# An attention and mixture-of-experts layer: the router's last steps, the order of its sends, and the last batch's additions re-timed

## The chip, the cores and the metric

The kernel runs on one core of a Trainium2 chip. The time is that of the whole program on the device, in microseconds (us); of the kernel before, three runs gave a median of 751.35 us (750.44 to 752.04). Five engines work side by side, each through its own instructions in a fixed order: PE multiplies matrices, DVE and ACT and POOL work on vectors, SP issues transfers. PE writes its products into PSUM; the others work in SBUF and PSUM; DMA moves rows between SBUF and the memory outside. An engine waits at an instruction until what it needs is there, and all that stands behind it on that engine waits too.

## The reference

The input `x` holds 16 batches of 512 rows of 128 numbers. With `xn = layernorm(x)` the output is `x + attention(xn) + experts(xn)`.

```python
q, k, v = heads of xn@Wq, xn@Wk, xn@Wv          # 16 heads of 8 numbers
q, k = q/|q|, k/|k|
attn = softmax(causal(8 * q k^T))
attention = (attn v) @ Wo

probs = softmax(xn @ Wr^T)                      # 8 experts
top_v, top_i = top_k(probs, 2); top_v /= sum(top_v)
experts = sum over e of  w_e * (gelu(xn @ W1[e]^T + b1[e]) @ W2[e]^T + b2[e])
```

Here `w_e` is the weight that a row gives to expert `e`, zero if it is not one of the row's two. All numbers are 32-bit floats.

## The kernel before, in words

**The stages of attention.** A batch's attention goes in 10 stages (`PER`), so that the program has stages 0 to 159 (`PER * B` = 160), and stage t belongs to batch t // 10. In each stage PE makes the scores of four heads at once (`scores`, L727), ACT takes the exponentials (L737), POOL or DVE sets to zero what lies above the diagonal (`mask`), and two stages later (`LAG`) PE weighs the values with them (`weigh`, L771) into `av`, the one PSUM buffer for it. After four stages in ten, at t % 5 of 4 and 1, DVE transposes `av` into SBUF (L783); the next weighing writes the same buffer and waits for that. `prep` has the steps that make the next batches' queries and keys (among them L624 `proj`, L683 `qT`, L690 `kr`, L696 `kT`), and `finish` those behind the weighing: division by the sums (L798, L800), a transpose (L810), the product with `Wo` into `po` (L815), the addition to `x` (L819). `prep`, `finish` and others enter their steps in `plan` under a stage number. The products that need one small PSUM buffer (`misc`: `proj`, the turned `q` and `k`, `po`, idle products) share it, one at a time.

**The order of the work.** PE, SP, DVE and ACT execute in the order in which the program's text issues instructions, and `on_pool` holds POOL to the same. `stage(t, b, n)` issues, in this order: at most two sends, the scores, a step of `side`, the masks of the stage before, the weighing, and then `due(t)`: the steps of `plan` for t, the router's steps whose stage has come, one of the steps in `later`, and calls of `combine`.

**The router.** From stage 20 on `route` and `place` run as 19 steps on DVE, with a product or a few on PE: the best and second-best expert of each row, their weights, and for each of the two choices the position at which the row is to lie among its expert's rows. The table of stages ahead of `stage` names them by index: 7 to 9 are `exps`, `shares` and `gates` (which writes the weights into the last columns of the rows), 10 to 16 are `taken`, `count`, `starts`, `ends`, `earlier`, `slot` and `moved`, 17 and 18 are `choose(0)` and `choose(1)`, which write the positions. Behind them come 13 steps in `later` (`ended`, `owners`, `own`, `bias`, `biased`), which find out which expert owns which block of rows; one goes at each stage with t % 10 of 3, 4 or 8.

**The sends.** From stage 40 on POOL sends the rows to `slots`, in the memory outside: 128 indirect transfers of 128 rows, 13 in each batch's ten stages (line 565 is the helper's, for all that POOL does).

**The experts.** Behind stage 139 (`FIRST` = 14 batches) the 71 blocks of rows are fetched, multiplied (L884, L897), weighted and scattered to `results`. Batch 13 is weighed to its end beside the first of them, and batch 14 begins behind the last.

**The last two batches.** From stage 140 on attention goes on for batches 14 and 15. Between, SP loads the experts' results of each batch (`bring`, into buffers called `xnT` and `yt`), `combine(b)` adds them to `x` on DVE in two additions of 128x512 (L983), and `store` sends a batch to `out` when both the attention's and the experts' share have been added. `late` lists the batches that wait for `combine`; `due` starts them by a rule of t: from stage 145 one per stage, two at 148, 153 and 158, none at 151. After stage 159, two more stages (160, 161) weigh what is left, each with one idle product (`keep_busy`, L1031, 128x384 of the weights `wall`, whose result nobody reads), then four idle products follow, and the last batch's division, transpose, product, addition and store.

## Time and profile before

| what | value |
|---|---|
| median of three runs | 751.35 us (750.44 to 752.04) |
| the profiled execution | 748.66 us |
| its span in the profile | 747.0 us |
| PE, DVE, ACT, POOL busy | 716.7, 474.0, 469.0, 475.1 us |
| weighing that waits for DVE's transpose (L783), after us 130 | 6.5 us in 7 waits |
| POOL's sends (128, line 565, `slots<-rows,pos`) | 149.8 us |
| attention up to the experts; experts; the last two batches | to about 425; about 425 to 687; about 687 to 747 us |

The page's times are microseconds from the start of the span. PE, DVE, ACT and POOL are the engines; SP issues transfers. A line such as `734.27 1.48 PE L771 MATMUL av<-ex,vaug 128*12 128x512 f32 x16 [1.93 <-DVE mid L783]` reads: from 734.27 us on, for 1.48 us, PE ran 16 passes for line 771 of the kernel, which write `av` and read `ex` and `vaug`; before that it stood idle for 1.93 us, until DVE's line 783, which writes `mid`, was done. A 32-bit product is two passes. Matmuls are pipelined and their ends are modelled. The profiled execution is one; its own time stands beside the median of the other runs.

### The profile page before, as it was taken

The page shows a single profiled execution, that of the slowest core. Times are in us where ns is not written, and L with a number is a line of the kernel's source. Part 1 is how long each engine was busy: PE and PEld are TensorE (multiplying, and loading weights), DVE is VectorE, ACT ScalarE, POOL GpSimd, SP SyncE. Part 2 cuts the span into 40 slices and gives each one's busy share as a digit, 9 for nine tenths or more (in the row PEclk, how much of TensorE's full clock was granted, in tenths as well). Part 3 has the DMA queues.
Part 4 walks back from the last instruction along what each step waited for, and adds up shares of the span by engine and source line. Part 5 has one row for each costly group of instructions (what it writes and reads, how often), then busy time and mean ns, then how long its engine had stood idle before and what let it go on. Part 6 is the DMA issues. An engine that isn't in the chain of part 4 may idle for free.

```text
span 747.0 us, 17437 instructions
## 1 busy us (share of the span) xinstructions
PE 716.7 (96%) x6411; PEld 437.9 (59%) x6411; DVE 474.0 (63%) x1045; ACT 469.0 (63%) x732; POOL 475.1 (64%) x565
## 2 busy tenths in 40 slices
PE   6899999989999999999999899999999999999996
PEld 2344544334444344444444489999899999998442
DVE  6875578897877876667666645554545554444694
ACT  3677677768887788788888734444343444446872
POOL 4658355478898888888888436554545455455542
PEclk9999999999999999999999999999999999999999
DMA  9930000001101101111110488878778877871992
GB/s 264 342 126 2 1 1 2 1 21 37 35 30 35 37 32 33 38 33 34 35 37 31 133 259 248 238 239 235 226 209 235 241 236 225 248 214 35 296 328 58
DMA packets 90358, 95.38 MB, mean 128 GB/s; under 512 B 10765, under 2 KB 67984, under 8 KB 90274
## 3 DMA queue, kind: packets, MB, share of 16 engines
q1 hardware_dynamic: 80994, 76.93, 35.4%
q0 software_dynamic: 8416, 17.06, 6.7%
q8 instruction: 51, 0.84, 0.5%
q10 hardware_dynamic: 864, 0.28, 0.2%
q14 instruction: 33, 0.27, 0.1%
HBM read 63.87 MB, written 30.82 MB: 127 GB/s over the span
## 4 chain that ended last, share of the span: by engine, by line
PE 78%; DVE 11%; POOL 6%; issue 3%; DMA 1%; ACT 1%; DVEq 0%; POOLq 0%; ACTq 0%
PE sim L727 16%; PE av L897 16%; PE av L771 16%; PE ph L884 16%; PE proj L624 5%; POOL slots L565 3%; PE xgt L861 2%; DVE x L983 2%; PE po L815 2%; PE idle L1031 2%; DMA xnT<-results 1%; POOL ex L565 1%; DVE mid L783 1%; PE qt L681 1%; PE xnt L296 1%
## 5 line engine op out<-in xcount | busy, mean ns | idle before, releaser
L737 ACT ACTIVATE ex<-sim 128x1024 f32<-128x1024 f32 x320 | 310.0, 1022 | 89.3 <-PE sim L727 86.3
L565 POOL DMA_INDIRECT results<-y,to x135 | 132.6, 982 | 132.7 <-DVE y L905 108.9
L888 ACT ACTIVATE gT<-ph,bias 128x256 f32<-128x256 f32 x284 | 108.5, 465 | 150.5 <-PE ph L884 145.4
L727 PE MATMUL sim<-qT,kT 32*128 32x512 f32 (+3 forms) x2048 | 189.6, 460 | 0.5 <-ACT ex L737 0.5
L771 PE MATMUL av<-ex,vaug 128*12 128x512 f32 (+3 forms) x2048 | 168.2, 435 | 8.0 <-DVE mid L783 7.3
L565 POOL DMA_INDIRECT slots<-rows,pos x128 | 149.8, 1171 | 29.5 <-issue 25.8
L565 POOL TENSOR_SCALAR_AFFINE_SELECT ex<-ex 128x512 f32<-128x512 f32 (+1 forms) x139 | 113.9, 826 | 78.6 <-ACT ex L737 73.1
L727 PEld LDWEIGHTS sim<-qT,kT 32*128 32x128 f32 x2048 | 95.8, 183 | 77.2 <-issue 34.3
L897 PE MATMUL av<-xnT,gT 128*128 128x128 f32 x1080 | 132.4, 275 | 0.9 <-ACT gT L888 0.9
L884 PE MATMUL ph<-xgT,xnT 128*128 128x256 f32 (+1 forms) x568 | 129.0, 370 | 2.3 <-DVE xgT L864 2.3
L897 PEld LDWEIGHTS av<-xnT,gT 128*128 128x128 f32 x1080 | 126.3, 192 | 2.5 <-ACT gT L888 1.9
L771 PEld LDWEIGHTS av<-ex,vaug 128*12 128x12 f32 x2048 | 42.4, 91 | 118.8 <-issue 82.8
L884 PEld LDWEIGHTS ph<-xgT,xnT 128*128 128x128 f32 x568 | 99.2, 191 | 13.3 <-DVE xgT L864 2.9
L783 DVE STREAM_TRANSPOSE mid<-av 128x512 f32<-128x512 f32 x64 | 45.7, 714 | 62.5 <-PE av L771 62.3
L864 DVE COPY xgT<-xgt 128x256 f32<-128x256 f32 x71 | 29.2, 411 | 63.4 <-PE xgt L861 63.4
L902 DVE TENSOR_TENSOR y<-av,bb 128x256 f32<-128x256 f32 x71 | 29.2, 411 | 63.0 <-PE av L897 60.8
L624 PE MATMUL proj<-wall,xnT 128*128 128x384 f32 x128 | 57.6, 536 | 6.4 <-DVE xnT L297 2.9
L749 DVE TENSOR_TENSOR ex<-ex,causal 128x1024 f32<-128x1024 f32 (+1 forms) x43 | 53.8, 1252 | 4.7 <-ACT ex L737 4.6
L565 POOL TENSOR_TENSOR qkn<-qkv 128x256 f32<-128x256 f32 x64 | 42.8, 677 | 10.7 <-ACT qkv L627 10.3
L624 PEld LDWEIGHTS proj<-wall,xnT 128*128 128x128 f32 x128 | 19.3, 188 | 33.1 <-issue 16.3
L696 DVE TENSOR_SCALAR kT<-kr,hmask 128x512 f32<-128x512 f32 x64 | 37.9, 595 | 0.6
L627 ACT COPY qkv<-proj 128x384 f32<-128x384 f32 x64 | 30.9, 482 | 9.7 <-PE proj L624 8.3
(162 smaller groups left out, 553.2 us busy)
## 6 DMA issues: line engine op xcount, KB each, us to landing
xnT<-in_w1T_dram SPq DMA_DIRECT2D x71, 256.0 KB
xnT<-in_w2T_dram SPq DMA_DIRECT2D x71, 256.0 KB
slots<-fill SPq DMA_DIRECT2D x45, 198.0 KB, 5.0
xg<-slots SPq DMA_DIRECT2D x64, 132.0 KB
xnT<-results SPq DMA_DIRECT2D x13, 512.0 KB, 8.5
bb<-in_b_dram SPq DMA_DIRECT2D x71, 64.0 KB, 3.5
x<-in_x_dram SPq DMA_DIRECT2D x16, 256.0 KB, 4.9
out_dram<-x SPq DMA_DIRECT2D x16, 256.0 KB, 4.0
```

Of the source, the lines that this page charges most:

```text
L565: ins = op(*args, **kw)
L624: nc.tensor.matmul(pp[:, :NQKV], xnT[b][:, ts(c, P)], wall, start=True, stop=True)
L627: nc.scalar.copy(s["qkv"][:, c], pp[:, :NQKV])
L696: nc.vector.tensor_scalar_mul(s["kT"][:, r], s["kr"], hmask[:, r : r + 1])
L727: nc.tensor.matmul(halves[g // 2][:, g % 2, col : col + (NC - j) * P], s["kT"][group, r, ts(j, P)], s["qT"][group, j * P :], start=True, s ...
L737: nc.scalar.activation(ex[:, 2 * h : 2 * h + 2], half, AF.Exp, scale=SCALE)
L749: nc.vector.tensor_mul(diag, diag, causal.unsqueeze(1).unsqueeze(1).to_broadcast([P, NG, many, P]),)
L771: nc.tensor.matmul(av[32 * g : 32 * g + VW, j * P :], s["vaug"][:, j, NG * g + r], s[m][:, g, col : col + (NC - j) * P], start=(j == 0), s ...
L783: nc.vector.transpose(s["mid"][:, r], av)
L884: nc.tensor.matmul(ph[:, m], s["w1"][:, ts(m, P)], s["xgT"], start=True, stop=True)
L888: nc.scalar.activation(s["gT"][:, m], ph[:, m], AF.Gelu, bias=bias1[:, i, m : m + 1])
L897: nc.tensor.matmul(py[:, c], s["gT"][:, m, ts(c, P)], s["w2"][:, m], start=(m == 0), stop=(m == NM - 1),)
```

## The change: what it does

- `starts` (step 12) goes at stage 31 instead of 33; `gates` (step 9) at 38 instead of 37. `choose(1)` is no longer a step of the router but the first step of `later`, and is still issued at stage 38; so each of the 13 steps behind it goes one place later (the last at stage 83 instead of 78).
- `choose(k)` enters the 64 sends of its choice. So all the first choices' sends go first, then all the second choices'; before, each tile of 128 rows had both, one after the other. The stages and the number of sends in each are the same.
- The `combine`s have a new rule: from stage 145 one per stage, two at 147 and 159, none at 151 and 158, the last at 160.
- Of the idle products near the end, the one at stage 161 is dropped, and two instead of four stand ahead of the last product.
- For the last batch the addition and the store of the result go in two halves of 256 columns.

The transfers' bytes, the products that count, and what ACT and POOL do are the same.

```diff
             nc.vector.tensor_copy(pos[:, k], at)
-            if k:
-                sends.extend(
-                    lambda k=k, i=i: send(k, i) for i in range(NT) for k in range(2)
-                )
+            sends.extend(lambda i=i: send(k, i) for i in range(NT))
...
         return [
             taken, count, starts, ends, earlier, slot, moved,
-            lambda: choose(0), lambda: choose(1),
-        ], [lambda f=f, k=k: f(k) for k in range(2) for f in (ended, owners)] + [own] + [
+            lambda: choose(0),
+        ], [lambda: choose(1)] + [
+            lambda f=f, k=k: f(k) for k in range(2) for f in (ended, owners)
+        ] + [own] + [
             lambda f=f, m=m: f(m) for m in range(NM) for f in (bias, biased)
         ]
...
             xb = x_sb[b].rearrange("p c d -> p (c d)")
-            nc.vector.tensor_add(xb, po, xb)
-            store(b)
+            if b < B - 1:
+                nc.vector.tensor_add(xb, po, xb)
+                store(b)
+            else:
+                assert b in ready
+                for c in range(0, NC, 2):
+                    part = slice(c * P, (c + 2) * P)
+                    nc.vector.tensor_add(xb[:, part], po[:, part], xb[:, part])
+                    nc.sync.dma_start(
+                        out[b, part].rearrange("(c p) d -> p c d", p=P), x_sb[b][:, c : c + 2]
+                    )
             del live[b]
...
-        late[:0] = [(PER * FIRST + 5, n) for n in range(FIRST)]
+        late[:0] = [(PAIR, n) for n in range(FIRST)]
...
-        (29, (6,)), (30, (11,)), (31, (7,)), (32, (8,)), (33, (12, 13)), (34, (14,)),
-        (35, (15,)), (36, (16,)), (37, (17, 9)), (38, (18,)),
+        (29, (6,)), (30, (11,)), (31, (7, 12)), (32, (8,)), (33, (13,)), (34, (14,)),
+        (35, (15,)), (36, (16,)), (37, (17,)), (38, (9,)),
...
-        if b is None:
+        if t == PER * B:
             keep_busy(1, wall)
...
-        for _ in range(2 if t % PAIR == 3 else t % PER != 1):
+
+        t -= PER * FIRST
+        for _ in range(2 if t in (7, 19) else t not in (11, 18)):
             if late and late[0][0] <= t:
                 combine(late.pop(0)[1])
...
-    keep_busy(4, wall)
+    keep_busy(2, wall)
```

## The prediction

> **What bounds the kernel now.** I read the page first, then the waits of PE, then the timeline round the two places that the change touches: the router's end (us 150 to 160) and the last batch (us 700 to 747).

> The page's first part, and from the waits (engine, line, what it waited for, us in total, times, longest), PE's after us 130:

> ```profile
> PE 716.7 (96%) x6411; PEld 437.9 (59%) x6411; DVE 474.0 (63%) x1045; ACT 469.0 (63%) x732; POOL 475.1 (64%) x565
> ...
> PE av L771 <- DVE mid L783: 6.5, 7, 1.9
> PE proj L624 <- DVE kr L690: 1.6, 1, 1.6
> ```

> PE is the bound almost throughout, so only PE's stalls and the tail behind its last product can be won. DVE causes most stalls: the next weighing (L771) may not write `av` before DVE has transposed it (L783), and DVE's strict order puts other work ahead of that. The largest are these (timeline: start, length, in brackets the idle time before):

> ```profile
> 151.91 0.21 DVE L377 TENSOR_TENSOR sums<-wsel 128x64 f32<-128x64 f32 x1
> ...
> 154.02 0.68 DVE L690 COPY kr<-kt 128x512 f32<-128x512 f32 x1
> ...
> 156.68 0.74 DVE L501 TENSOR_TENSOR past<-iota_b,end 128x568 f32<-128x568 f32 x1
> 157.34 0.71 DVE L783 STREAM_TRANSPOSE mid<-av 128x512 f32<-128x512 f32 x1
> ...
> 154.75 0.91 PE L624 MATMUL proj<-wall,xnT 128*128 128x384 f32 x2 [1.55 <-DVE kr L690]
> 158.19 1.48 PE L771 MATMUL av<-ex,vaug 128*12 128x512 f32 x16 [1.46 <-DVE mid L783]
> ```

> The gates (five instructions from 151.91) hold up `kr`, and `past` holds up the transpose. At the end:

> ```profile
> 728.35 5.15 DVE L983 TENSOR_TENSOR x<-x,xnT 128x512 f32<-128x512 f32 x6
> 733.42 0.71 DVE L783 STREAM_TRANSPOSE mid<-av 128x512 f32<-128x512 f32 x1
> 737.65 0.72 DVE L783 STREAM_TRANSPOSE mid<-av 128x512 f32<-128x512 f32 x1 [3.52 <-PE av L771]
> ...
> 739.25 0.71 DVE L810 STREAM_TRANSPOSE oT<-o 128x512 f32<-128x512 f32 x1
> 742.59 0.69 DVE L819 TENSOR_TENSOR x<-po,x 128x512 f32<-128x512 f32 x1 [2.63 <-PE po L815]
> ...
> 734.27 1.48 PE L771 MATMUL av<-ex,vaug 128*12 128x512 f32 x16 [1.93 <-DVE mid L783]
> ...
> 737.51 3.82 PE L1031 MATMUL idle<-wall 128*128 128x384 f32 x8
> 741.39 1.16 PE L815 MATMUL po<-wo_sb,oT 128*128 128x128 f32 x8
> ```

> Six additions (three of `combine`) delay the transpose at 733.42 by 1.8 us and PE by 1.93. `oT` is ready at 739.96, but the last product starts at 741.39: it stands behind four idle products.

> **The change part by part.** The profiled execution took 748.66 us (span 747.0); the median shown is 751.35, so 2.69 more. I sum against the span and carry the difference to the median.

> *`starts` at stage 31.* Five small instructions, 135.30 to 136.59, 1.3 us, move ahead of L810 and `shares`. DVE runs without a gap from 129.16 to 141.9, so the transpose at 138.94 does not move, nor PE's 0.88 us stall there. What now comes 1.3 us later: `oT`, ready about 133.5, wanted at 136.69; `ss`, ready about 136.7, wanted by ACT at 138.12. Cost 0.

> *Gates behind `kr` and `kT`, `ended(0)` out of stage 38.* `kr` goes at 151.91 (its product ended at 151.5): PE's 1.55 us vanishes. But it then meets the transpose earlier: DVE has the same work before that, less `past`, 156.68 to 157.34. So of 1.55 only 0.66 us stays. POOL's first send waits for the gates: about 155.4 instead of 154.44. Behind it stand the second send, the squares at 158.28 and the masks. The second send now reads a first choice's position and no longer waits for 156.77, so two sends end near 158.1 instead of 158.25, and the rest of POOL's queue is not later. Gain 0.66; ends: 0 (POOL is on the chain from 193 to 244, and PE waits 0.71 for it at 244.00) and 1.0.

> *The other steps one slot later.* At stages 48 and 68 PE lost 0.28 (184.98) and 0.45 us (238.43) to a transpose behind four `owners` instructions (1.65) and one `bias` (1.55). Now one `past` (0.74) and one reduction (0.73) stand there, and a `bias` each moves into 58 and 78, worth 0 to 0.45 each. Between -0.73 and +0.17; I take -0.1, near the middle of new against old stalls.

> *Order of the sends.* 128 as before, at the same places between POOL's instructions, 1.17 us each, the same rows and bytes. SP reads slots only at stage 140. Cost 0; the row that bounds it is the sends' own 0.96 to 1.86 us, whose spread has no tie to the choice that I can see, so 0 with ±0.3.

> *Additions re-timed.* Up to stage 152 DVE's order is the same. At 153 one `combine` less stands before the transpose: it starts at 719.54 instead of 720.86, and PE's 0.51 at 721.71 goes. At 156 PE is the later one. At 159 two `combine`s less stand before it; it goes when PE is through, 731.0 (731.43+0.1, less 0.51 and rounding), ends 731.7, and PE's 1.93 goes: L771 starts at about 731.9, 2.4 earlier. Then the weighings follow, 1.42 and 0.98, with no idle product (0.84) between. POOL's last two masks (1.65 from 732.94) come 0.6 earlier and end at 734.0, so PE ends near 734.5 instead of 737.58.

> But three `combine`s now stand between the last two transposes, where none stood: six additions from 731.65. A pair took 1.32 us undisturbed (732.10 to 733.42) and 1.65 to 2.1 beside a mask (728.35 to 730.45). At 3 × 1.32 plus about 0.6 for the two masks they end at 736.15. So DVE, not PE, ends last: the last transpose starts 1.5 us before its 737.65, not 3.1. Ends: 3 × 1.32 gives 735.6; 3 × 2.1 gives 737.9. I take nearer the quiet rate, since POOL has only 1.65 us of work left.

> *Two idle products instead of four.* From the last transpose's start to `oT`'s end it took 2.31 us; so `oT` is ready at 738.5. PE's two idle products (1.9) end at 736.4, out of the way. The last product starts at 738.5 instead of 741.39: 2.9 us earlier (3.4 and 1.2 at the ends). All PE waits named before are in this sum.

> *Last addition and store in halves.* Both wait for the whole product, as the second addition brings no wait of its own. Two additions of 128x256 at 0.41 (L902's row) against one of 0.69: the second store goes 0.1 later than the one would. The old store took 2.30 us from issue (743.30) to landing (745.60); half the bytes land in between nothing saved and perhaps 0.4 less. Net 0, ±0.3; SP's queue is empty by then.

> Sum: 0.66 + 0.1 + 2.9 = 3.7 us. 747.0 becomes 743.3, the profiled execution about 745.0, the median 751.35 - 3.7 = 747.65; I say 747.7.

> [...] PE's granted clock is 1.00 in all windows to 740 and 0.92 in the last:

> ```profile
> 740.00:747.00 7.00, 2.44 (x12) 1.26 (x10) 0.69 (x1) 0.00 (x0) 0.00 (x0) 0.92 0.14 37
> ```

> 0.08 of 7.00 us is 0.56, at half clock 1.1 us, so the clock falls near 745.9, 3.4 us after PE's last product. At the start, at half clock, two passes of 512 columns took 2.09 us (L1031) against 1.05 later (L403), so a drop would double the last product's 1.16. My sum leaves PE idle for 2.1 us (736.4 to 738.5), about as long as the 1.93 before L771 at 734.27, behind which 16 passes ran at the usual 1.48: no cost. [...]

> The additions beside masks ran 1.00 to 1.47 instead of 0.69, and a mask of 1.08 ran 1.62. [...]

> **Rivals.** (1) *The gain stays in DVE's queue.* The six additions go at 2.1 a pair throughout, the last transpose starts at 737.9 and `oT` is ready at 740.2; the tail wins only 1.2, and if PE's idle time of 3.8 us lowers the clock, the product takes 1.2 more. The front's 0.76 is lost at 244. Then 751.35 - 0 to 1.2, say 750.7. For it: nearly all second additions between 716 and 732 took 1.0 to 1.47. Against: POOL is done by 734. (2) *POOL becomes the bound in front*: the first send is 0.96 later and POOL hands that on to 244, +0.96 instead of -0.76, so 749.4. Against it: POOL waited for ACT at 181.64 and 208.43, so it had caught up. (3) *Slower*: every one of the six additions takes 1.47 (the longest seen). The last transpose starts at 740.4, `oT` is ready at 742.7, PE has idled over 6 us, the product takes 2.3 and ends at 745.0 against 742.55: +2.45 - 0.76, 753.0. Its turning point is 1.23 us an addition, where `oT` is as late as the four idle products made the last product. (4) *The edits do nothing in front*, DVE's stretch staying full: 748.45, inside the forecast's own range.

> **How the numbers follow.** A measurement of this kernel tells about 0.2% (1.5 us) from no change. Forecast, with (4), 746.4 to 749.4: 0.70. (2): 0.08, also faster by over 0.2%. (1): 0.14, within 0.2%. (3): 0.06; other causes of a loss 0.02. So faster 0.78, same 0.14, slower 0.08. The range goes from the quiet additions with a full gain in front (3.4 + 1.0 + 0.5 = 4.9, 746.4) into (1), 750.7.

> **What would show it.** `proj` near 153.2 without a wait for `kr`; L771 at 157.5; no wait of PE for `mid` after 715 over 0.3 us; six additions of 4.0 to 5.2 us ending at 735.6 to 736.8 (0.8 earlier if the front's gain holds); the last product led by `oT`, not by idle products, at 1.16. Wrong I'd be if those additions went over 7 us, if the clock fell before the last product, or if PE's waits for POOL between 160 and 250 grew by over 1 us.

## The result, and the profile after

The changed kernel takes 744.88 us (median of four runs, 744.58 to 746.93) against 750.89 for the kernel before beside it; the ratio is 0.9941 with a 95% interval of 0.9917 to 0.9964, or 4.4 us less (2.7 to 6.2). Put to the 751.35 us of the runs shown, that is 746.9 us against a forecast of 747.7. The medians themselves lie 6.0 us apart, more than the forecast's range allowed; what is known of that rest stands further down. Ratios leave out the few executions that ran over 1.5% longer than the shortest of their kernel (the longest: 1761.92 us of the kernel before, 814.71 us of the one with `choose(1)` at stage 43, below). The profiled execution took 746.93 us, the longest of the four; the one before, 748.66, was shorter than all four runs beside it (748.99 to 752.04). So the spans, 745.2 against 747.0, differ by only 1.8 us.

The first part of its page, and the waits of PE after us 130 (engine, line, what it waited for, us in total, times, longest):

```profile
PE 716.9 (96%) x6405; PEld 438.8 (59%) x6405; DVE 474.8 (64%) x1046; ACT 468.6 (63%) x732; POOL 473.5 (64%) x565
```

```profile
PE av L770 <- DVE mid L782: 3.5, 3, 2.1
...
PE po L814 <- DVE oT L809: 2.0, 1, 2.0
PE av L770 <- POOL ex L564: 1.6, 5, 0.7
```

PE is still the bound. Its waits for `mid` fell from 6.5 us to 3.5, the wait for `kr` is gone, and one is new: the last product waits 2.0 us for `oT`. The router's end (timeline: start, length, idle time before in brackets):

```profile
149.80 0.68 DVE L689 COPY kr<-kt 128x512 f32<-128x512 f32 x1
...
151.02 0.91 PE L623 MATMUL proj<-wall,xnT 128*128 128x384 f32 x2
...
152.71 0.69 DVE L491 TENSOR_TENSOR mine<-xnT,sel 128x512 f32<-128x512 f32 x1
...
154.26 0.71 DVE L782 STREAM_TRANSPOSE mid<-av 128x512 f32<-128x512 f32 x1
...
155.12 2.24 PE L770 MATMUL av<-ex,vaug 128*12 128x512 f32 x16 [2.12 <-DVE mid L782]
```

`kr` now runs ahead of the gates and `proj` waits for nothing. But VectorE (DVE) then works through the gates and, as before, through `choose(1)` (from 152.71) ahead of the transpose, and PE reaches it earlier, so PE's next wait is 2.12 us instead of 1.46. The weighing behind it takes 2.24 us instead of the 1.48 it took before. The end of the last batch:

```profile
731.41 0.72 DVE L782 STREAM_TRANSPOSE mid<-av 128x512 f32<-128x512 f32 x1 [1.04 <-PE av L770]
732.06 4.78 DVE L991 TENSOR_TENSOR x<-x,xnT 128x512 f32<-128x512 f32 x6
...
735.36 1.88 PE L1039 MATMUL idle<-wall 128*128 128x384 f32 x4
...
736.75 0.71 DVE L782 STREAM_TRANSPOSE mid<-av 128x512 f32<-128x512 f32 x1
...
738.34 0.71 DVE L809 STREAM_TRANSPOSE oT<-o 128x512 f32<-128x512 f32 x1
...
739.20 1.89 PE L814 MATMUL po<-wo_sb,oT 128*128 128x128 f32 x8 [1.96 <-DVE oT L809]
741.12 0.76 DVE L825 TENSOR_TENSOR x<-po,x 128x256 f32<-128x256 f32 x2 [2.07 <-PE po L814]
741.58 0.89 SPq L826 DMA_DIRECT2D out_dram<-x  x2
```

The additions no longer delay the transpose at 731.41; it is VectorE that waits now (1.04 us). Six additions stand between the last two transposes and take 4.78 us. The last product is led by `oT`, with the idle products out of the way, but takes 1.89 us instead of 1.16.

Both slow pieces of PE's work lie in a stretch at half clock, as the windows show (stretch, length, then busy us of PE, PEld, DVE, ACT and POOL, each with its count; the granted clock of PE, DMA share, GB/s). The stretches are cut where the clock record changes:

```profile
152.29:155.70 3.41, 1.29 (x16) 0.28 (x12) 3.31 (x9) 2.59 (x4) 2.25 (x2) 1.00 0.06 22
155.70:159.11 3.41, 3.41 (x32) 1.42 (x20) 1.94 (x2) 0.00 (x0) 3.20 (x4) 0.50 0.07 24
...
735.97:739.38 3.41, 1.39 (x4) 0.51 (x4) 2.94 (x6) 0.00 (x0) 0.00 (x0) 1.00 0.29 77
739.38:742.79 3.41, 1.71 (x8) 1.41 (x7) 0.76 (x2) 0.00 (x0) 0.00 (x0) 0.50 0.09 25
```

After a window in which PE was idle for 2.1 and 2.0 of 3.41 us, the clock is half for the next one. A third such window (425.35 to 428.77) follows the experts' first transposes, behind one in which PE was idle for 1.92 us. The kernel before had waits at the same places, but its windows fell otherwise, or the idle time in them was less:

```profile
151.99:155.40 3.41, 1.86 (x26) 0.77 (x18) 3.27 (x9) 1.98 (x3) 2.82 (x4) 1.00 0.03 7
155.40:158.82 3.42, 1.96 (x17) 0.59 (x20) 3.35 (x7) 2.42 (x3) 2.00 (x3) 1.00 0.07 22
...
732.26:735.67 3.41, 1.48 (x17) 0.39 (x16) 1.83 (x3) 0.55 (x1) 1.65 (x2) 1.00 0.31 89
```

Its 1.55 us (for `kr`) and 1.46 us (for `mid`) were in two windows, and the 1.93 us ahead of 734.27 did not lower the clock.

So that the clock's chance windows can be told from the edits, I cut every span at three PE rows: the weighing behind a wait of 0.77 us at 123 to 125 (start of part B), the experts' first transpose `xgt` behind 1.06 us (start of C), and the weighing behind the last batch's wait of 1.0 us (start of D). Part B holds the router's end and all the sends, C the experts, D the last batch's end. The starts in the changed kernel are 123.10, 423.55 and 709.68. "Half" marks a window at half clock in that part.

| | A | B | C | D | span |
|---|---|---|---|---|---|
| before | 124.49 | 300.25 | 284.51 | 37.70 | 747.0 |
| after | 123.10 | 300.44 half | 286.13 half | 35.54 half | 745.2 |

Before and after, C is the same work: 1.62 us is what one half-clock window costs. The sum is -1.39 in A, +0.19 in B, +1.62 in C and -2.16 in D. A has no edit in it; PE's clock became full at 12.04 us before and at 8.93 after, and over all 14 profiles A is longer where that was later (123.1 us for 8.9, 123.5 for 9.6 to 9.9, 124.5 for 12.04). So that is chance too.

### The profile page after: what moved, and what is told of

It reads as the page before. It is cut to its first block, busy times and chain, and to the rows that moved or that the text cites. A ratio compares the mean times of both kernels' runs of the same rounds, so it can differ in the third digit from the quotient of the medians.

```text
span 745.2 us, 17428 instructions
## 1 busy us (share of the span) xinstructions
PE 716.9 (96%) x6405; PEld 438.8 (59%) x6405; DVE 474.8 (64%) x1046; ACT 468.6 (63%) x732; POOL 473.5 (64%) x565
## 3 DMA queue, kind: packets, MB, share of 16 engines
q1 hardware_dynamic: 81010, 76.93, 35.2%
## 4 chain that ended last, share of the span: by engine, by line
PE 84%; DVE 8%; POOL 4%; ACT 2%; issue 2%; DMA 1%; DVEq 0%; POOLq 0%; ACTq 0%
PE sim L726 19%; PE av L770 17%; PE av L905 16%; PE ph L892 16%; PE proj L623 6%; PE po L814 2%; POOL slots L564 2%; PE xgt L869 2%; DMA xnT<-results 1%; PE qt L680 1%; DVE x L991 1%; PE idle L1039 1%; PE kt L687 1%; ACT ex L736 1%; PE xnt L296 1%
## 5 line engine op out<-in xcount | busy, mean ns | idle before, releaser
L564 POOL DMA_INDIRECT slots<-rows,pos x128 | 146.4, 1144 | 29.2 <-issue 25.9
L564 POOL TENSOR_TENSOR qkn<-qkv 128x256 f32<-128x256 f32 x64 | 45.0, 712 | 9.3 <-ACT qkv L626 9.0
```

The source lines that it names most:

```text
L564: ins = op(*args, **kw)
```

## The experiments

**The two halves of the change, and the two parts of the tail.** These ran on another chip, where the experts' part takes 13 to 18 us longer and the times scatter more (the kernel before: 763.54 us, 757.65 to 773.73).

The front alone is the kernel before with the new order of sends, the later steps and the table:

```diff
-            if k:
-                sends.extend(lambda k=k, i=i: send(k, i) for i in range(NT) for k in range(2))
+            sends.extend(lambda i=i: send(k, i) for i in range(NT))
...
-            lambda: choose(0), lambda: choose(1),
+            lambda: choose(0),
+        ], [lambda: choose(1)] + [
...
-        (29, (6,)), (30, (11,)), (31, (7,)), (32, (8,)), (33, (12, 13)), (34, (14,)),
-        (35, (15,)), (36, (16,)), (37, (17, 9)), (38, (18,)),
+        (29, (6,)), (30, (11,)), (31, (7, 12)), (32, (8,)), (33, (13,)), (34, (14,)),
+        (35, (15,)), (36, (16,)), (37, (17,)), (38, (9,)),
```

> Only the router's steps, the sends' order and the later steps are changed; the end is as before. Theory (DVE's order): PE loses its waits for kr and for two transposes, and gains one smaller wait; between us 100 and 420 PE comes 0.7 to 1.6 us ahead of before, and the median is 0.7 to 1.6 us lower, 0.1 to 0.2%. Rival A (the clock's phase makes most of the change): PE's order wins nothing lasting, under 0.4 us at us 420 when windows of half clock are taken out. Rival B (POOL hands its late first send on): PE is 0.3 to 1.0 us later than before at us 250.

The tail alone is the kernel before with the re-timed additions, the idle products and the halves; then come the idle products alone, and the additions alone:

```diff
-    keep_busy(4, wall)
+    keep_busy(2, wall)
...
-        if b is None:
+        if t == PER * B:
```

```diff
-        late[:0] = [(PER * FIRST + 5, n) for n in range(FIRST)]
+        late[:0] = [(PAIR, n) for n in range(FIRST)]
...
-        for _ in range(2 if t % PAIR == 3 else t % PER != 1):
+        t -= PER * FIRST
+        for _ in range(2 if t in (7, 19) else t not in (11, 18)):
```

> Only the last batch's part is changed: additions, idle products, halves; the router is as before. Theory: the last product starts 2.5 to 2.9 us earlier against PE's events at us 700, it is led by the last transpose, and the median falls by 2.2 to 3.0 us, 0.3 to 0.4%; if PE's idle time before the last product falls into a window of the clock, that product takes 1.9 instead of 1.2 us. Rival A (the gain stays in DVE's queue): under 1.5 us.

> Before, with the idle product of stage 161 and two of the last four taken out, nothing else. Theory: in before the last product stood behind the idle products 1.4 us after oT was ready, and one more delayed the last weighing by 0.84, so this alone wins about 2.2 us (the last transpose 0.84 earlier, the last product 0.05 behind oT); with additions moved as well the two gains overlap, since then DVE ends last. If the additions were what counts, under 0.5 us.

> Before, with the additions' stages alone changed; all six idle products stay. Theory: PE's waits of 0.51 and 1.93 go, the six additions end 1.0 to 1.5 us before the last transpose of before, and four idle products end near oT, so this alone wins about 2.2 us, too, and the last product runs at full clock because PE is not idle ahead of it (1.17 us). If the idle products were what counts, under 0.7 us.

| | ratio | 95% | median, us | B | C | D |
|---|---|---|---|---|---|---|
| front | 0.9990 | 0.9961 to 1.0019 | 761.40 | 303.39 half | 302.29 | 37.69 |
| tail | 0.9936 | 0.9909 to 0.9964 | 758.44 | 301.35 | 302.19 | 35.19 half |
| idle products | 0.9962 | 0.9937 to 0.9988 | 761.56 | 302.38 | 298.96 | 35.41 |
| additions | 0.9971 | 0.9938 to 1.0004 | 760.34 | 301.90 | 297.62 | 35.29 |

The times say that the gain is the tail's. They can say little more, since C differs by 5 us between executions without an edit in it. The lead of 0.7 to 1.6 us that the front was to gain is not to be seen: its B is 1.0 to 2.0 us longer than with the front untouched, with a half-clock window of 1.62 in it. Part D says more: the front leaves it at 37.69, and each half of the tail takes 2.3 to 2.4 us from it. Together they take 2.5 here, where the last product lay partly at half clock (1.54 us), so the two overlap for the most part. With fewer idle products only, the additions still delay the transpose, but PE catches up, since no idle product stands between the last weighings, and `oT` leads by 0.70 us:

```profile
749.55 0.71 DVE L783 STREAM_TRANSPOSE mid<-av 128x512 f32<-128x512 f32 x1
750.40 2.34 PE L771 MATMUL av<-ex,vaug 128*12 128x512 f32 x32 [1.92 <-DVE mid L783]
...
755.26 1.13 PE L815 MATMUL po<-wo_sb,oT 128*128 128x128 f32 x8 [0.70 <-DVE oT L810]
```

With the additions only, the wait of 1.93 us is gone, but the last product stands behind four idle products again:

```profile
745.61 1.48 PE L771 MATMUL av<-ex,vaug 128*12 128x512 f32 x16
...
748.84 3.83 PE L1031 MATMUL idle<-wall 128*128 128x384 f32 x8
...
751.67 0.71 DVE L810 STREAM_TRANSPOSE oT<-o 128x512 f32<-128x512 f32 x1
...
752.73 1.16 PE L815 MATMUL po<-wo_sb,oT 128*128 128x128 f32 x8
```

`oT` ends at 752.38 and the idle products at 752.67.

**The changed kernel again, and the clock at its end.** On a quieter chip (the kernel before: 752.22 us) I ran the changed kernel once more, without an edit.

> The changed kernel once more, unaltered, beside three kernels that differ from it in one place each. From the first pair of traces: the stretch from the weighing that follows PE's wait of 1.0 us (first of the last batch's waits for `mid`) to the end of the span, 37.75 us before the change and 35.5 after it, is again 35 to 35.6 us here (35.5 where PE's 1.96 us of idle time ahead of the last product lies in one window of the clock gate, 34.8 where it is split). PE's wait for `mid` behind choose(1) is again 2.1 us. Against the kernel before: 3.5 to 5 us lower. A rival, that the front cost what the tail won, expects less than 2 us.

Measured: 746.32 us, ratio 0.9919 (0.9890 to 0.9947), 5.9 us between the medians, more than the 3.5 to 5 expected; B 301.73 with a half-clock window, C 286.15 with one, D 35.65 with the last product at half clock (2.01 us). D as expected. The wait at the router's end was 2.12 us again, split between two windows this time (1.66 us in one), and no drop followed it; it followed a wait of 1.88 us for POOL at 242.98 instead.

Then one idle product more at the end:

```diff
-    keep_busy(2, wall)
+    keep_busy(3, wall)
```

> The changed kernel with three idle products at the end instead of two. Theory on the clock: the last product ran at half clock (1.87 instead of 1.17 us) because PE was idle for 1.96 us within one 3.41 us window ahead of it. One more idle product (0.95 us) leaves 1.0 us idle; the clock stays full until the last product in every execution, the product takes 1.17 us, and the last product still starts right behind `oT`. The stretch to the end is 34.8 us whatever the phase of the window: 0.7 us less than the changed kernel's where that drops, the same where it does not. Rival: the product was slow for another reason (its eight weights are `oT`, loaded late), and takes 1.87 us again.

Measured: 745.38 us (744.93 to 746.46), ratio 0.9911 (0.9885 to 0.9938), B 300.42 and C 286.14 with a half-clock window each, D 34.78. The end of its timeline:

```profile
735.66 2.85 PE L1039 MATMUL idle<-wall 128*128 128x384 f32 x6
...
738.64 0.71 DVE L809 STREAM_TRANSPOSE oT<-o 128x512 f32<-128x512 f32 x1
739.50 1.13 PE L814 MATMUL po<-wo_sb,oT 128*128 128x128 f32 x8 [0.99 <-DVE oT L809]
```

PE is idle for 0.99 us, the product starts right behind `oT` as before, and takes 1.13 us. D is 0.76 us shorter than after the change and 2.92 shorter than before it. That the clock, and not weights that come late, made it 1.89 us, another profile of the tail shows best. With the sends interleaved (below), PE waits the same 1.96 us for `oT`, but 1.60 of it lie in one window and the rest in the next, the clock stays full, and the product takes 1.13 us:

```profile
747.91 1.13 PE L817 MATMUL po<-wo_sb,oT 128*128 128x128 f32 x8 [1.96 <-DVE oT L812]
```

So the rival is out. In the times, 0.76 us is not to be seen.

**`choose(1)` out of the transpose's way.** It goes at stage 43 instead of 38, and all later steps one place further:

```diff
-        if later and not router and t % PER in (3, 4, 8):
+        if later and not router and t > 38 and t % PER in (3, 4, 8):
```

> The changed kernel, but with choose(1) at stage 43 instead of 38, out of VectorE's work ahead of the transpose of stage 39; ended, owners, bias and biased each go one place later still. My theory, that PE's wait at that transpose grew from 1.46 to 2.12 us because `choose(1)` stands ahead of it (1.55 us): the wait becomes 0.5 to 0.7 us, no half-clock window can follow it, and the span is 1.5 us shorter than the changed kernel's, up to 3.1 where that one's wait fell into one clock window. Rival: the weighing then waits for POOL (masks behind sends) or the later stages' transposes give the 1.5 us back by us 270: no difference to the changed kernel within 0.5 us.

```profile
153.60 0.71 DVE L782 STREAM_TRANSPOSE mid<-av 128x512 f32<-128x512 f32 x1
...
154.45 1.48 PE L770 MATMUL av<-ex,vaug 128*12 128x512 f32 x16 [0.57 <-DVE mid L782]
```

Measured: 743.06 us, ratio 0.9881 (0.9852 to 0.9911); B 299.67 and C 284.51, neither with a half-clock window, and D 35.50, with the last product at half clock (1.84 us). The wait is 0.57 as expected, and the weighing takes 1.48 us again. But of the 1.55 us, and of the window of 1.62 that no longer follows, B keeps 0.77 against the first profile of the changed kernel, 2.06 against the second. Its waits for POOL between 128 and 300 tell where the rest went:

```profile
PE av L770 <- POOL ex L564: 3.3, 5, 1.1
```

They were 1.2 in the first profile of the changed kernel and 2.8 in the second: PE, earlier by the wait that it no longer has, meets the masks behind POOL's sends. So both theories hold a part. The profiled execution took 745.37 us, though; four others took 743.00 to 743.08, below all six of the changed kernel beside them (743.95 to 749.38). Where those four are shorter was not traced.

**The last additions spread as well**, on top of `choose(1)` at 43:

```diff
-        for _ in range(2 if t in (7, 19) else t not in (11, 18)):
+        for _ in range(2 if t == 7 else t != 11):
```

> As the kernel with choose(1) at stage 43, and the last additions spread so that one `combine` each goes at stages 158, 159 and 160, where the changed kernel has none at 158 and then one and two more behind. Theory: VectorE stood idle for 1.04 us ahead of the transpose at 731.4, so a pair of additions (1.35 us) there puts PE's wait for that transpose up by 0.3 us and the last transpose down by 1.0 us; `oT` is ready 1.0 us earlier, PE is idle for 0.5 to 1.0 us ahead of the last product, which goes at full clock (1.17 us). The stretch from the first weighing of the waits named above to the end is 34.0 to 34.6 us instead of 35.5; in all 2.5 us below the changed kernel (1.8 to 4.0). Rival: the added pair meets a mask of POOL and takes 2.1, the transpose is late by 1.1, and nothing is won at the end.

```profile
728.59 0.70 DVE L782 STREAM_TRANSPOSE mid<-av 128x512 f32<-128x512 f32 x1
...
729.45 2.42 PE L770 MATMUL av<-ex,vaug 128*12 128x512 f32 x32 [0.59 <-DVE mid L782]
...
732.59 0.71 DVE L782 STREAM_TRANSPOSE mid<-av 128x512 f32<-128x512 f32 x1
...
735.04 1.13 PE L814 MATMUL po<-wo_sb,oT 128*128 128x128 f32 x8 [1.36 <-DVE oT L809]
```

Measured: 744.31 us (741.97 to 747.79), ratio 0.9910 (0.9875 to 0.9945); the profiled execution took 742.04 with a span of 740.3 (B 298.36, C 284.51, D 33.97). D falls as expected: the first transpose goes without idle time ahead of it, PE waits 0.59 us there, four additions instead of six stand before the last one, and the product goes at full clock. Its profiled execution is the shortest of all. By times it is not told apart from the changed kernel or from `choose(1)` at 43 alone: the three intervals overlap.

**Front and tail once more, the order of the sends, the last store in one piece.** The first two are the kernels of the first experiment, unchanged; the last two are the changed kernel with

```diff
-            sends.extend(lambda i=i: send(k, i) for i in range(NT))
+            if k:
+                sends.extend(lambda k=k, i=i: send(k, i) for i in range(NT) for k in range(2))
```

and with

```diff
-            if b < B - 1:
-                nc.vector.tensor_add(xb, po, xb)
-                store(b)
-            else:
...
+            nc.vector.tensor_add(xb, po, xb)
+            store(b)
```

> The kernel before with the router's and the sends' edits alone, once more, beside the kernels that share its parts. I cut the span into four: to the first weighing after the stretch without waits (about us 124), from there to the experts' first transposes (300.3 us before, 300.4 after the change), from there to the first waits of the last batch (284.5 us where no half-clock window falls in it, 286.1 with one), and the rest (37.75 before, 35.5 after). Theory: PE's 1.55 us ahead of `proj` is gone, PE's wait at the next transpose is 2.1 us instead of 1.46, and the whole wait lies in one window of the clock gate in about half of the executions, which then takes 1.6 back; so the second part is 298.8 without that window and 300.4 with it, the last part stays at 37.7, and the time is 0 to 1.5 us below the kernel before. Rival: the spread router alone is worth 3 us or more, since the changed kernel's median lies 6 us below the other's and its last part only 2.3.

> The kernel before with the last batch's edits alone (additions, idle products, halves), once more. Theory: the last part 35.2 to 35.6 us instead of 37.75, the second part as before (300.3, with one or no wait of over 1 us for POOL), and the time 2.2 to 2.9 us lower. Rival: the remaining 3 us of the medians' difference come from here too, and the time is 5 us lower.

> The changed kernel with the sends interleaved again (each block's first choice, then its second). The second send of stage 40 waits for choose(1)'s last position again, at about 154.3 instead of being free. The forecast on record: 0 within 0.3 us. A rival: POOL loses 0.3 to 1.4 us there, hands it on through squares and masks until us 300, and PE waits for POOL longer in the second part, 0.5 to 1.5 us more; and since an instruction that waits differs from execution to execution, the times scatter by 4 us as those of the kernel before, where the changed kernel's mostly lie within 2.

> The changed kernel with the last addition and store in one piece again. The forecast on record: 0 within 0.3 us. In the changed kernel the two additions took 0.42 and 0.41 and the second store landed 1.9 us after its issue, in the kernel before 0.69 and 2.30; so one piece should cost 0.2 us (2.30 - 1.9 = 0.4 of landing, less 0.1 of addition and 0.1 of the second issue): the last part is 35.7 instead of 35.5 at the same clock, which the times cannot tell. Rival: the halves win over 0.5 us, as half the bytes are on their way 0.5 us earlier.

They met a scattering chip again (the kernel before: 762.85 us, 758.62 to 770.62):

| | ratio | 95% | median, us | B | C | D |
|---|---|---|---|---|---|---|
| front | 0.9982 | 0.9952 to 1.0012 | 762.86 | 301.27 half | 298.45 | 37.69 |
| tail | 0.9958 | 0.9929 to 0.9988 | 760.48 | 302.00 | 296.89 | 34.77 |
| after, sends interleaved | 0.9926 | 0.9894 to 0.9959 | 757.79 | 299.82 | 294.92 | 34.78 |
| after, one piece | 0.9977 | 0.9947 to 1.0006 | 760.50 | 302.40 half | 292.99 | 35.05 |

The front is 0.1 to 0.2% both times, with intervals that hold no change and nearly 0.5%; the tail is 0.4 here. D is 34.77 or 34.78 wherever the last product went at full clock with the change's additions and the halves, and 35.05 in one piece: the halves are worth 0.27 us. Interleaved sends cost nothing that shows: PE waits for POOL not once in B, and the time is no higher. So the rival's cost in B falls; whether the order changes the scatter cannot be told on a chip where every kernel scatters. The medians of the last two rows differ by 2.7 us, their profiled executions (754.88 and 755.63) by 0.8: B is 2.6 longer in the second, 1.6 of it a half-clock window, and C 1.9 shorter. Between kernels without an edit in C it differs as much, so the times cannot weigh these two edits.

## Why the prediction was right, and where it was not

*The tail.* The forecast had -2.9 for additions and idle products and 0 ± 0.3 for the halves. Measured in D: -2.92 at full clock for all three, of which 0.27 is the halves, so -2.65 for the first two; in the profile of the change itself -2.16, because of the next step. The other steps came as told: no wait of PE for `mid` after 715, six additions in 4.78 us (4.0 to 5.2 was said) that end at 736.84 (to 736.8, but 0.43 us of it is the later start of D), `oT` leading the last product. Rival (1), additions at 2.1 a pair, is out: a pair took 1.59 on average.

*The last product at 1.16.* This step failed, and with it came a sign that the forecast itself had named for being wrong: the clock fell before the last product. I argued that 2.1 us of idle time are harmless, since 16 passes ran at full clock behind 1.93 us. In the first two profiles of the changed kernel the clock fell and the product took 1.89 and 2.01 us; with the idle time at 0.99 it took 1.13. What I missed is where the window lies: of the seven profiles with 1.96 us of idle time ahead of the last product, the three in which two windows shared it kept the full clock (D 34.78 with the sends interleaved), and in four the clock fell. It cost 0.76 and 0.87 us in the changed kernel's two.

*`kr` ahead of the gates.* The forecast had 0.66 us, which means a next wait of 2.35 (1.46 + 0.89). The 1.55 us went and PE's next wait grew to 2.12: 0.89 won. But the wait of 2.12 us lowered the clock for the next window in five of the seven profiles that have it, and this takes 1.62 back. Nothing of it was in the sum. In the second profile of the changed kernel it was a wait of 1.88 for POOL at 242.98 that lowered the clock; there PE's waits for POOL between 160 and 250 were 2.3 us in all, against 0.7 before, which is another sign that the forecast had named.

*`starts` at stage 31, cost 0.* Mis-sized: the wait of 0.88 us is gone. I said that the transpose at 138.94 would not move, having only put the same durations in another order. They are not the same where POOL works beside them. VectorE's rows before and after:

```profile
133.46 0.54 DVE L373 TENSOR_TENSOR wsel<-wsel,sums 128x128 f32<-128x128 f32 x1
...
135.30 0.17 DVE L425 TENSOR_SCALAR many<-tot 128x8 int32<-128x8 f32 x1
135.50 0.64 DVE L426 TENSOR_SCALAR left<-many 128x8 int32<-128x8 int32 x1
...
138.45 0.57 DVE L458 TENSOR_TENSOR move<-move,room 128x8 f32<-128x8 f32 x1
138.94 0.70 DVE L783 STREAM_TRANSPOSE mid<-av 128x512 f32<-128x512 f32 x1
```

```profile
129.98 0.60 DVE L425 TENSOR_SCALAR many<-tot 128x8 int32<-128x8 f32 x1
130.61 0.32 DVE L426 TENSOR_SCALAR left<-many 128x8 int32<-128x8 int32 x1
...
133.29 0.29 DVE L373 TENSOR_TENSOR wsel<-wsel,sums 128x128 f32<-128x128 f32 x1
...
136.74 0.17 DVE L458 TENSOR_TENSOR move<-move,room 128x8 f32<-128x8 f32 x1
136.83 0.71 DVE L782 STREAM_TRANSPOSE mid<-av 128x512 f32<-128x512 f32 x1
```

From the transpose before to this one, the same work took 9.78 us before (from 129.16) and 9.06 after (from 127.77), and PE's wait of 0.88 us at 139.79 is gone in all nine profiles with this edit (at most 0.16, for POOL, stands there). Of the 0.72 us, 0.54 lie in the four instructions shown. POOL's rows show what differs: 138.45 (L458) before stands beside a mask that runs from 138.36 to 139.00, and ends 0.02 us behind it; at 136.74 after, no POOL row stands beside it. L425 goes the other way: it now stands beside a mask, and is longer.

*The front as a whole.* Forecast: 0.76. B of the kernel before was 300.25; after the change it is 300.44 with a half-clock window, which leaves 298.8 without; the second profile, 301.73, leaves 300.1. With the front untouched, B on the scattering chips was 301.35, 302.38, 301.90 and 302.00, none with such a window; with it changed 303.39, 301.27, 302.40, each with one, and 299.82 without. Less 1.62 for each window, that is 1.4 us won on average there; on the quieter chips it is 1.4, 0.1 and, with three idle products (300.42), 1.4. The clock takes 1.6 back in six of these seven profiles. The front alone measured 0.9990 and 0.9982, both within 0.2%. That the forecast's size was near is luck: its errors, waits that shrank more than it said and a clock that it left out, cancel. Rival (2), POOL becoming the bound, is not what the first profile shows (waits for POOL of 1.2 us against 0.7 up to us 300), though it cost the second one its 1.88 us and held back the kernel with `choose(1)` at 43.

*Order of the sends, 0 ± 0.3.* No cost or gain was to be seen.

*The other steps one slot later, 0.1 won.* In the first profile PE's two waits of 0.28 and 0.45 us are gone, and one of 0.34 at 263.86 is new: 0.4 won. The second has none of the three; with the sends interleaved there are two, of 0.29 and 0.63.

*What stays open.* The traced parts account for some 3 us: 2.2 to 2.9 in D and about 0 in B. The ratio gives 4.4 (2.7 to 6.2) and, the second time, 6.1 (4.0 to 8.3). Part of the rest is the choice of executions: the profiled one of the kernel before is at the low end and has no half-clock window ahead of its last product, and the profiled one of the changed kernel is the longest of its four and has three. The mean granted clocks of the other runs (1 is full clock throughout) point the same way. The changed kernel's other three, 1.8 to 2.4 us shorter, have 0.996 against 0.992, some 6 us less at half clock, or about two windows; at 1.62 each, an estimate, that is 3.2. Of the kernel before, on the second quiet chip, the shortest run (748.48) has 0.999 and the longest of the usual ones (754.88) 0.993. So windows that fall by chance can move a time by as much as the edits do, and a median of four holds some of that. How much of the rest is chance and how much the edits' is not shown, since each of those runs has no trace. The two tails alone measured 0.9936 and 0.9958, 3.2 to 4.8 us, so they take part of it, but within intervals that also hold 2.9.

## What to carry to other kernels

Where a wait of the bounding engine is removed, look at the one that it is merged into: the two waits of 1.55 and 1.46 us cost their own length, the one of 2.12 us cost 1.62 more in five of seven profiles. Idle products belong only where they end before their successor is ready, but there they are worth having: one more at the end saved 0.76 us against the profile in which the clock fell, while in the kernel before they held up the last product by 1.4 us. Where an engine's small instructions stand beside another's long ones, their durations are not to be carried over to another order: L458 took 0.57 us in one and 0.17 in the other. And where executions of one kernel differ by more than an edit is worth, cut the span at fixed rows and compare the parts: D reproduced to 0.01 us over three chips (37.70, 37.69, 37.69 without the tail's edits) while the medians moved by 13 us.

## What the runs showed of the hardware that was not expected

Small VectorE instructions took over three times as long in one place as in another. In all 14 profiles L458 (128x8) took 0.17 us in the nine in which no POOL row stood beside it and 0.56 or 0.57 in the five in which a mask did; for L373 (128x128) it is 0.29 and 0.54, for L425 0.16 or 0.17 and 0.60. In the two profiles, before and after, the four rows of 128x8 behind us 100 that begin while a POOL row runs (L425 after, L426 in both, L458 before) end 0.02 to 0.03 us behind the end of a POOL row, as if they waited for it. No run moved POOL's masks alone, so this is shown by where the rows stand, not by an experiment.

The experts' part, the same in all these kernels, took 284.5 to 286.2 us on the quieter chips and 293 to 302 on the two others, with up to four half-clock windows in it.
